# Attention in a convolution block: the last row-sum addition of a group behind the group's eviction, group-norm steps and position sums at other places

## The chip, the core and the metric

The kernel runs on one core of one Trainium2 chip. Its time is the device time of one execution in microseconds (us), the median of three runs; lower is better. The core has a matrix engine (TensorE, PE in the profile, with its weight loads as PEld), a vector engine (VectorE, DVE), a scalar engine (ScalarE, ACT), a general engine (GpSimd, POOL) and a queue engine (SyncE, SP). Each engine works through its own instructions in the order in which they were built, and waits on semaphores for the others.

## The reference

The input is 8 images of 512 channels, 32 x 32 positions, float32. The layer is a group norm, a block of convolutions with two attentions in it, and a residual:

```python
t = cbs(x, cv1_w, cv1_bn, 0)                 # 1x1 convolution, batch norm, silu
ys = [t[:, :C], t[:, C:]]                    # C = 256
for i in range(N):                           # N = 2 blocks
    yi = ys[-1]
    z = cbs(yi, m_cv1_w[i], m_cv1_bn[i], 1)  # 3x3 convolution
    z = bot_attention(z, m_qkv_w[i], m_rw[i], m_rh[i])
    z = silu(bn_eval(conv2d(z, m_cv2_w[i], 0), m_cv2_bn[i]))
    ys.append(yi + z)
return cbs(concatenate(ys, axis=1), cv2_w, cv2_bn, 0)
# bot_attention: 4 heads of 64 channels over 1024 positions
q, k, v = conv2d(x, qkv_w, 0)
r = rw + rh                                  # position sums, one 1024-vector per channel
a = softmax(einsum('bhdi,bhdj->bhij', q, k + r) * HD ** (-0.5))
out = einsum('bhij,bhdj->bhdi', a, v)
# whole layer: x + block(group_norm(x))
```

## The kernel before

The 8 images are worked on in four **rounds** (`p` = 0 to 3) of two images, a **first** and a **second** one. A round runs the 3x3 convolution of block 0 for both images, then project and attention of the first image, then of the second, and the same for block 1, and then the last 1x1 convolution. That makes 16 attentions, each by `attention_fast`. While they run, the other engines prepare what comes next: the group norm of the next round's images, tiles of the next convolution, weights for later rounds.

**One attention** has 4 groups (two heads by one half of the query positions); a group has 8 tiles of 128 keys, taken two at a time, so 4 steps. In a step PE makes the logits of two key tiles (L1037, `l_ps`), ACT the exponentials (L1041, `pt`), DVE adds them up over the keys into `acc` (L1055 for the first two tiles of a group, L1057 after that), and PE multiplies the step before by v into `av_ps` (L1071). At the end of a group ACT copies one half of `av_ps` into `z` (L1078) and DVE adds the other half to it (L1079): this is the **eviction**. There is one buffer for `av_ps`, so the next group's first product with v waits for it.

A **border** is the place between two groups, border 1 to 3 in each attention. There the engines' orders are: PE makes the logits of the new group's first step, the products with v of the old group's last step, the logits of the new group's second step, and then the products with v of the new group's first step. DVE does the old group's last additions, the eviction, and the new group's first addition L1055.

**Sums.** The softmax's denominators are the sums of `acc` over the partitions, made by PE with a matrix of ones (L1089, `s_ps`). In most attentions groups 0 and 1 are summed together at border 2, ahead of the products with v of group 2's first step, and groups 2 and 3 after the attention. Five attentions (both of round 0's block 0, and the second image's of block 0 in rounds 1 to 3) sum group 2 alone at border 3 as well. `acc` has two buffers.

**Hooks.** `behind` maps a place in the attention, group or (group, step), to a function that issues some instruction of other work behind that step's addition. `NORM_A` is the list of places at which the next round's first image goes through a step of its group norm (`group_norm`) during the first image's block 0 attention of rounds 1 and 2: four steps of statistics (DVE, L718 and L719), one for the mean over a group of channels (two small matmuls on PE, L725 `gm_ps`, then DVE L734 to L737), one for the deviation (`gv_ps`), and four that scale a tile of x (ACT, L809).

**Position sums.** `make_r(0)` adds `rw` and `rh` into four tiles (DVE, L217) and stores them to HBM from the POOL queue (L221). They are read by the projections of block 0 from round 1 on. Round 0 issues them in `middle()`, between the two images' attentions of block 1, with DVE's work of the second image's projection (L989 to L1006).

`tc.issue_after(ins)` makes what is issued inside it stand behind `ins`; a scheduler sets the rest of each engine's order when the program is built.

Of the kernel before, what the change touches and what calls it, by code (L numbers as in the profile page):

```python
# [47 lines left out]
ALU = mybir.AluOpType  # L48
# [13 lines left out]
def kernel(  # L62
# [16 lines left out]
    nc = tc.nc  # L79
# [7 lines left out]
    NJ = HW // P  # L87
# [121 lines left out]
    def make_r(n, raw=None):  # L209
        if raw is not None:  # L210
            with tc.issue_after(s.last_exp[0].ins):
                turn_r(n, raw)
            yield
        for c in range(NM):
            for half in range(NH):
                r = act.tile([P, ROWS, F], F32, tag="t", name="r_new", bufs=4)
                tt(  # L217
                    r, rw_sb[:, n, c].unsqueeze(1).to_broadcast([P, ROWS, F]),
                    rh_sb[:, n, c, ts(half, ROWS)].unsqueeze(2).to_broadcast([P, ROWS, F]), ALU.add,
                )  # L220
                put_r[0] = nc.gpsimd.dma_start(r_dram[n][c][:, ts(half, HALF)], r.rearrange("p h w -> p (h w)"))  # L221
                yield
# [268 lines left out]
    def stages(act, small, ps_big, ps_av, n_pt):  # L491
# [522 lines left out]
        def attention_fast(qkv, ao, at, behind, at_once=False, apart=False):  # L1014
# [4 lines left out]
            groups = [(c, half) for c in range(NM) for half in range(NH)]  # L1019
            steps = [(g, j) for g in range(len(groups)) for j in range(NJ)]  # L1020
            PAIR = 2
            pairs = [steps[i : i + PAIR] for i in range(0, len(steps), PAIR)]
            pts, accs, avs = {}, {}, {}

            def logits(pair):
                g, j0 = pair[0]
# [23 lines left out]
            def add_up(pair):  # L1050
                g, j0 = pair[0]
                pt = pts[pair[0]]
                if j0 == 0:
                    accs[g] = act.tile([P, 2, HALF], F32, tag="acc", name="acc", bufs=2)
                    return nc.vector.tensor_tensor(accs[g], pt[0], pt[1], ALU.add)  # L1055
                for i in range(PAIR):
                    ins = nc.vector.tensor_tensor(accs[g], accs[g], pt[i], ALU.add)  # L1057
                return ins

            def times_v(pair):  # L1060
# [95 lines left out]
            s_drams, rss, evicted = {}, {}, [None]  # L1156
            for i in range(len(pairs) + 1):
                if i < len(pairs):
                    added = logits(pairs[i])
                    g, at_q = divmod(i, NQ)  # L1160
                    with tc.issue_after(added.ins):
                        if at_q == NQ - 2 and g - 1 in batch:
                            gs = batch[g - 1]
                            rss[gs] = spread(gs, s_drams[gs])
                        if i == 1:
                            later()
                        if at_q == 1 and g - 2 in batch:
                            scale_all(batch[g - 2])
                if i > 0:
                    g, j0 = pairs[i - 1][0]  # L1170
                    if j0 == 0 and g - 1 in batch:
                        s_drams[batch[g - 1]] = sums(batch[g - 1])
                    times_v(pairs[i - 1])
                    if i < len(pairs) and accs.get(pairs[i][0][0], 0) is None:
                        with tc.issue_after(evicted[0].ins):
                            before = behind.get(("border", pairs[i][0][0]), lambda: None)() or evicted[0]
                        with tc.issue_after(before.ins):
                            added = add_up(pairs[i])
                    with tc.issue_after(added.ins):
                        behind.get(g if j0 == 0 else (g, j0 // PAIR), lambda: None)()  # L1180
# [3 lines left out]
            g = len(groups) - 1  # L1184
            if not at_once:
                gs = batch[g]
                if apart:
# [3 lines left out]
                    evicted=evicted[0], added=added,  # L1191
# [492 lines left out]
    with tc.issue_after(first.ins), tc.issue_after(made.ins):  # L1684
        multiplied, _, applied, powered = next(norm)
# [149 lines left out]
    for p in range(NP):  # L1835
# [125 lines left out]
                        calls[key].append(extra[key])  # L1961
            return {key: (lambda fs: lambda: [f() for f in fs])(fs) for key, fs in calls.items()}

        NORM_A = ((0, 1), (0, 3), (1, 1), (1, 2), 2, (2, 1), (2, 2), (2, 3), 3, (3, 1))
        NORM_B = ((0, 1), (0, 3), (1, 1), (1, 2), 2, (2, 1), (2, 2), (2, 3), 3, (3, 1), (3, 2), (3, 3))
        extra = {}
        if p == 0:
# [4 lines left out]
            r_steps = make_r(1, load_r(1))  # L1972
# [3 lines left out]
        behind = hooks(() if p == 0 else NORM_A, {0: 2} | {i: 1 for i in range(1, 9)}, extra) | {NG: begin_cv1(0, Y1[0], ia + 2)}  # L1976
        if p == 0:
            behind[NG + 1] = lambda: nxt.go_on()
        end = s.attention_fast(qkv, z[:, :, 0], at_of(ia, 0), behind, at_once=p == 0)
# [115 lines left out]
        behind = hooks(NORM_B, {0: 1, 1: 1, 4: 1}, {key: step_part for key in at_keys})  # L2095
# [81 lines left out]
        behind = {NG: start_b}  # L2177
# [15 lines left out]
        def middle():  # L2193
            end.spread()
            end.scale()
            s.m2(1, z[:, :, 0], Y2[0], lambda oc, half: img(y3a[half][:, oc, :]))
            if p == 0:
                with tc.issue_after(end.evicted.ins):
                    for _ in make_r(0):
                        pass  # L2200
            if more:
                nxt.finish()
                nxt.keep()
            s.exp_table()
# [6 lines left out]
        if p == 0:  # L2211
            ws = {name: load_ws(name) for name in ("21", "22", "11", "12")}
            new, sums1, sums2 = make_ws(ws)
# [27 lines left out]
        a1, a1_more, a2, a3 = s.strassen(ia, w_of, top, tags_a, tile_of)  # L2241
        behind = {NG: a1}
        if p == 0:
            behind |= {0: sums1, 1: sums2}
        end = s.attention_fast(qkv, z[:, :, 1], at_of(ib, 1), behind)
        y3b = act.tile([P, NH, NM, HALF], F32, tag="v", name="y3b")
        end.sums()
# [134 lines left out]
```

## Time and profile before

| | |
|---|---|
| time, median of 3 runs | 2251.07 us (2250.76 to 2251.08) |
| profiled execution, from the first to the last instruction (span) | 2246.8 us |
| PE busy | 2200.9 us (98%) |
| DVE busy | 1728.7 us (77%) |
| ACT busy | 1099.6 us (49%) |
| POOL busy | 224.4 us (10%) |
| granted TensorE clock, mean | 0.999 |
| chain that ended last | PE 85%, DVE 11%, ACT 1%, issue 1%, DMA 1% |

The profile is of one execution. Its span is 4.3 us under the median of the timed runs, which also hold what lies before the first and behind the last instruction. A row of the timeline gives the start in us from the span's start, the duration in us (of all instructions merged into the row), engine, line, operation, output<-inputs, shapes and count, and in brackets how long the engine stood idle before it and what ended that. A row of the waits gives who waited for what, us in total, times, and the longest in us. Matmul rows overlap: a float32 matmul shows as two records, and the ends are modelled, so the time that PE needs is read from start to start.

### The profile page before, as it was taken

How to read it: one execution, taken by the hardware profiler on the slowest of the kernel's cores; microseconds unless marked ns; L12 is line 12 of the kernel's file. 1: busy time of each engine (PE TensorE's matmuls, PEld its weight loads, DVE VectorE, ACT ScalarE, POOL GpSimd, SP SyncE). 2: the span in 40 equal slices, each digit the busy share in tenths (PEclk: the TensorE clock that was granted, in tenths of full speed). 3: DMA queues.
4: the chain of work that ended last, by engine and by line, in shares of the span. 5: the costliest groups of instructions: out<-in, count | busy, mean ns of one | idle time of the engine just before them, and what ended most of it. 6: DMA issues, size and time to landing. Idle time of an engine off the chain costs nothing.

```text
span 2246.8 us, 40264 instructions
## 1 busy us (share of the span) xinstructions
PE 2200.9 (98%) x16346; PEld 1080.6 (48%) x16346; DVE 1728.7 (77%) x2648; ACT 1099.6 (49%) x1332; POOL 224.4 (10%) x417
## 2 busy tenths in 40 slices
PE   7999999999999999999999999999999999999998
PEld 3653437343474444634447343654344734473443
DVE  7988879878678688877857868986794868797652
ACT  7554653644225665456324666455622455335533
POOL 4322210000220000000021000000012000000001
PEclk9999999999999999999999999999999999999999
DMA  9854447321581324511257141532136611350214
GB/s 273 308 163 150 150 151 261 109 78 45 140 275 49 118 81 145 183 58 67 67 159 261 30 169 35 197 116 77 58 76 173 233 39 34 102 198 30 67 50 112
DMA packets 134309, 285.60 MB, mean 127 GB/s; under 512 B 33540, under 2 KB 61184, under 8 KB 133092
## 3 DMA queue, kind: packets, MB, share of 16 engines
q1 hardware_dynamic: 102212, 197.34, 26.7%
q0 software_dynamic: 31904, 85.61, 13.3%
q8 instruction: 131, 2.15, 0.4%
q14 instruction: 62, 0.51, 0.1%
HBM read 214.86 MB, written 68.03 MB: 126 GB/s over the span
## 4 chain that ended last, share of the span: by engine, by line
PE 85%; DVE 11%; issue 1%; ACT 1%; DMA 1%; SPq 0%; POOL 0%; DVEq 0%; ACTq 0%; POOLq 0%
PE av_ps L1071 18%; PE l_ps L1037 18%; PE c L1305 9%; PE c_ps L653 7%; PE c_new L1305 6%; PE p_ps L916 6%; PE ps L523 5%; PE m_ps L1285 5%; PE x_ps L1405 4%; PE p_ps L922 3%; PE s_ps L1089 1%; DVE acc L1057 1%; DVE c_e L680 1%; PE p_ps L886 1%; DVE c_t L673 1%
## 5 line engine op out<-in xcount | busy, mean ns | idle before, releaser
L1041 ACT ACTIVATE pt<-l_ps 128x1024 f32<-128x1024 f32 x512 | 495.5, 1023 | 332.1 <-PE l_ps L1037 218.8
L1057 DVE TENSOR_TENSOR acc<-acc,pt 128x1024 f32<-128x1024 f32 x384 | 469.6, 1223 | 44.6 <-ACT pt L1041 16.2
L1071 PE MATMUL av_ps<-pt,vT 64*64 64x512 f32 x4096 | 484.8, 590 | 5.2 <-DVE z L1079 4.9
L1037 PE MATMUL l_ps<-q,kr 64*64 64x512 f32 x4096 | 486.3, 590 | 3.0 <-ACT pt L1041 1.9
L1071 PEld LDWEIGHTS av_ps<-pt,vT 64*64 64x64 f32 x4096 | 156.3, 133 | 284.8 <-issue 233.5
L1037 PEld LDWEIGHTS l_ps<-q,kr 64*64 64x64 f32 x4096 | 157.5, 133 | 273.2 <-issue 247.0
L653 PE MATMUL c_ps<-v_in,u 128*64 128x128 f32 x4320 | 239.1, 273 | 2.5 <-issue 2.5
L653 PEld LDWEIGHTS c_ps<-v_in,u 128*64 128x64 f32 x4320 | 235.8, 137 | 9.4 <-issue 9.4
L1285 PE MATMUL m_ps<-z,m_sb 128*128 128x512 f32 x256 | 114.1, 593 | 0.0
L658 ACT COPY c_m<-c_ps 128x512 f32<-128x512 f32 x48 | 28.0, 584 | 170.1 <-PE c_ps L653 140.8
L916 PE MATMUL p_ps<-t_z,sq 128*128 128x512 f32 x224 | 107.0, 595 | 0.0
L1079 DVE TENSOR_TENSOR z<-av_ps,z 128x512 f32<-128x512 f32 x64 | 44.1, 689 | 79.1 <-ACT z L1078 79.1
L1055 DVE TENSOR_TENSOR acc<-pt 128x1024 f32<-128x1024 f32 x64 | 78.0, 1219 | 18.0 <-PE s_ps L1089 11.2
L495 ACT ACTIVATE t<-m_ps,bh,sh 128x512 f32<-128x512 f32 x64 | 46.3, 773 | 91.2 <-PE m_ps L1285 91.2
L916 PE MATMUL p_ps<-z,sq 128*128 128x512 f32 x168 | 80.1, 604 | 5.3 <-ACT z L495 5.2
L1355 POOL DMA_DIRECT2D c_out<-in_x_dram x56 | 50.2, 954 | 293.2 <-ACT c_out L495 288.5
L1285 PEld LDWEIGHTS m_ps<-z,m_sb 128*128 128x128 f32 x256 | 47.8, 190 | 56.8 <-issue 52.5
L1147 DVE TENSOR_TENSOR z<-z,rs 128x512 f32<-128x512 f32 x64 | 42.3, 686 | 27.4 <-DMA rs<-r_dram 27.2
L495 ACT ACTIVATE c_out<-cz,bh,sh 128x512 f32<-128x512 f32 x14 | 16.8, 1301 | 89.1 <-DVE cz L1382 89.1
L495 ACT ACTIVATE z<-z,bh,sh 128x512 f32<-128x512 f32 x64 | 47.6, 804 | 25.8 <-DVE z L704 25.2
L1405 PE MATMUL x_ps<-t_x,sw 128*128 128x512 f32 x128 | 55.9, 592 | 0.0
L922 PEld LDWEIGHTS p_ps<-sq,z 128*128 128x128 f32 x336 | 42.7, 191 | 26.6 <-issue 12.7
(313 smaller groups left out, 3143.4 us busy)
## 6 DMA issues: line engine op xcount, KB each, us to landing
u<-u SPq DMA_DIRECT2D x135, 512.0 KB, 4.8
rs<-r_dram SPq DMA_DIRECT2D x126, 128.0 KB, 3.1
sq<-sq SPq DMA_DIRECT2D x42, 384.0 KB, 5.9
x<-in_x_dram SPq DMA_DIRECT2D x28, 512.0 KB, 7.0
r_in<-r SPq DMA_DIRECT2D x28, 512.0 KB, 4.9
y_in<-y SPq DMA_DIRECT2D x28, 512.0 KB, 4.4
c_out<-in_x_dram POOLq DMA_DIRECT2D x56, 256.0 KB, 5.1
out_dram<-c_out POOLq DMA_DIRECT2D x56, 256.0 KB, 3.3
```

Of the source, the lines that this page charges most:

```text
L495: silued[0] = nc.scalar.activation(dst, src, AF.Silu, scale=sh[:, k : k + 1], bias=bh[:, k : k + 1])
L523: last_product[0] = nc.tensor.matmul(ps[:, half, :], w_of(k), rhs_of(k, half), start=(k == begin), stop=(k == end))
L653: conv_product[0] = nc.tensor.matmul(to[o], us[cp][:, k, row, c, o], rhs, start=(k == 0), stop=(k == NM - 1),)
L916: nc.tensor.matmul(ps[:, o, :], w[:, o, :], rhs, start=not onto, stop=True, skip_group_check=onto)
L922: nc.tensor.matmul(v[:, ts(j, P)], rhs[:, ts(j, P)], w[:, 2, :], start=j == 0 and not onto, stop=True, skip_group_check=True,)
L1037: nc.tensor.matmul(ps[kh * HD : (kh + 1) * HD, hd, :], kr[r, c, o : o + HD], q[r, c, ts(half, HALF)], start=True, stop=True,)
L1041: last_exp[0] = exp = nc.scalar.activation(pt, ps, AF.Exp, scale=SCALE)
L1057: ins = nc.vector.tensor_tensor(accs[g], accs[g], pt[i], ALU.add)
L1071: nc.tensor.matmul(avs[g][hd * HD : (hd + 1) * HD, kh, :], vT[r, j, o : o + HD], pt[i][r, hd, :], start=(j == 0), stop=(j == NJ - 1),)
L1285: nc.tensor.matmul(pss[half][:, oc, :], m2_sb[:, n, k, ts(oc, P)], ao[:, k, ts(half, HALF)], start=(k == 0), stop=(k == NM - 1),)
L1305: nc.tensor.matmul(ps[:, o, :], w[:, k, ts(o, P)], rhs[part][:, c], start=(k == 0 and not onto), stop=(k == KB - 1), skip_group_check=onto,)
L1405: nc.tensor.matmul(ps[:, o, :], w[:, c, ts(o, P)], rhs[c], start=(c == 0 and not onto), stop=(c == 1), skip_group_check=onto,)
```

## The change

Three edits:

1. In `add_up` and at the borders: the last of a group's additions (the second key tile of step 4) is no longer issued with the other one, ahead of the eviction, but behind the eviction and ahead of the new group's first addition. This holds for groups 0 to 2 of each attention, 48 places in all. The last group of an attention keeps the old order.
2. `NORM_A`: the fourth statistics step goes from step 2 to step 3 of group 1, which puts it behind border 2, and the four scaling steps go one place later each. Mean and deviation keep their places.
3. `make_r(0)` leaves `middle()`; its four steps are hooks in round 0's last attention (second image, block 1), at (1,2), 2, (2,2) and 3.

```diff
-            pts, accs, avs = {}, {}, {}
+            pts, accs, avs, last_pt = {}, {}, {}, {}
...
-                for i in range(PAIR):
+                held_back = j0 + PAIR == NJ and g + 1 < len(groups)
+                for i in range(PAIR - held_back):
                     ins = nc.vector.tensor_tensor(accs[g], accs[g], pt[i], ALU.add)
+                if held_back:
+                    last_pt[g] = pt[-1]
                 return ins
...
                         with tc.issue_after(evicted[0].ins):
-                            before = behind.get(("border", pairs[i][0][0]), lambda: None)() or evicted[0]
+                            before = nc.vector.tensor_tensor(accs[g], accs[g], last_pt.pop(g), ALU.add)
+                        with tc.issue_after(before.ins):
+                            before = behind.get(("border", pairs[i][0][0]), lambda: None)() or before
                         with tc.issue_after(before.ins):
                             added = add_up(pairs[i])
...
-        NORM_A = ((0, 1), (0, 3), (1, 1), (1, 2), 2, (2, 1), (2, 2), (2, 3), 3, (3, 1))
+        NORM_A = ((0, 1), (0, 3), (1, 1), (1, 3), 2, (2, 1), (2, 3), 3, (3, 1), (3, 2))
...
             s.m2(1, z[:, :, 0], Y2[0], lambda oc, half: img(y3a[half][:, oc, :]))
-            if p == 0:
-                with tc.issue_after(end.evicted.ins):
-                    for _ in make_r(0):
-                        pass
             if more:
...
         if p == 0:
-            behind |= {0: sums1, 1: sums2}
+            r_steps = make_r(0)
+            behind |= {0: sums1, 1: sums2} | {at: lambda: next(r_steps) for at in ((1, 2), 2, (2, 2), 3)}
```

What the built programs' orders show (line numbers shift: the held-back addition is L1179, L1057 becomes L1058, L1079 becomes L1082, L1089 becomes L1092):

PE's order and SP's are the same in both programs. Of DVE at border 2 of round 1's first image, block 1 (acc: row sums, pt: exponentials, z: attention output, rc: reciprocals of the sums), before:

```order
L1057 TENSOR_TENSOR acc<-acc,pt 128x1024 x2
L1079 TENSOR_TENSOR z<-av_ps,z 128x512
L1055 TENSOR_TENSOR acc<-pt 128x1024
L1057 TENSOR_TENSOR acc<-acc,pt 128x1024 x4
L1131 RECIPROCAL rc<-sums_all 128x16
```

and now:

```order
L1058 TENSOR_TENSOR acc<-acc,pt 128x1024
L1082 TENSOR_TENSOR z<-av_ps,z 128x512
L1179 TENSOR_TENSOR acc<-acc,pt 128x1024
L1055 TENSOR_TENSOR acc<-pt 128x1024
L1058 TENSOR_TENSOR acc<-acc,pt 128x1024 x4
L1134 RECIPROCAL rc<-sums_all 128x16
```

One of the two additions ahead of the eviction now stands behind it, as the last one that `s_ps` needs.

In the first image's block 0 attention of round 1 (st, mv: statistics of x; gm: mean over a channel group), DVE from border 2 on is now as follows; before, the two BN_STATS and the BN_AGGR stood ahead of the eviction:

```order
L1058 TENSOR_TENSOR acc<-acc,pt 128x1024
L1082 TENSOR_TENSOR z<-av_ps,z 128x512
L1179 TENSOR_TENSOR acc<-acc,pt 128x1024
L1055 TENSOR_TENSOR acc<-pt 128x1024
L718 BN_STATS st<-x 128x6 x2
L1058 TENSOR_TENSOR acc<-acc,pt 128x1024
L719 BN_AGGR mv<-st 128x2
L1058 TENSOR_TENSOR acc<-acc,pt 128x1024
L734 COPY gm<-gm_ps 128x4
```

The last statistics, which `gm_ps` on PE reads, now come behind two more additions. ACT in the same attention from the end of group 2 on (L1041: exponentials, L809: scaling of x, COPY z: the eviction's first half), before:

```order
L1041 ACTIVATE pt<-l_ps 128x1024 x4
L809 ACTIVATE x<-x,shift,gr 128x1024
L1041 ACTIVATE pt<-l_ps 128x1024 x2
L809 ACTIVATE x<-x,shift,gr 128x1024
L1078 COPY z<-av_ps 128x512
L1041 ACTIVATE pt<-l_ps 128x1024 x2
```

and now:

```order
L1041 ACTIVATE pt<-l_ps 128x1024 x6
L809 ACTIVATE x<-x,shift,gr 128x1024
L1081 COPY z<-av_ps 128x512
L1041 ACTIVATE pt<-l_ps 128x1024 x2
L809 ACTIVATE x<-x,shift,gr 128x1024
L1041 ACTIVATE pt<-l_ps 128x1024 x2
```

Between the exponentials of group 2's last step and the copy of border 3 there is one scaling instead of two; the fourth scaling now stands behind the last exponentials and the load of the next function table.

DVE in the second image's projection of round 0, block 1 (r_new: position sums; kr, q, vT: operands of the coming attention), before; now the two L217 rows are gone from here, and the four additions stand one by one inside the attention that follows:

```order
L1293 TENSOR_TENSOR y_half<-t,ypad_67 128x512 x4
L217 TENSOR_TENSOR r_new<-rw_sb,rh_sb 128x512 x2
L989 TENSOR_TENSOR kr<-p_ps,u_z 128x512
L990 TENSOR_TENSOR q<-p_ps,u_z 128x512
L991 TENSOR_TENSOR vT<-p_ps,u_zv 128x4x128
L994 TENSOR_TENSOR kr<-kr,m_z 128x512
L217 TENSOR_TENSOR r_new<-rw_sb,rh_sb 128x512 x2
L995 TENSOR_TENSOR q<-q,m_z 128x512
```

## The prediction, made before the changed kernel was run

> **What bounds the kernel now.** I read the page first (busy times, clock, costliest groups), then PE's waits, then the timeline of PE, ACT and DVE around the borders and the moved work.
>
> ```profile
> span 2246.8 us, 40264 instructions
> PE 2200.9 (98%) x16346; PEld 1080.6 (48%) x16346; DVE 1728.7 (77%) x2648; ACT 1099.6 (49%) x1332; POOL 224.4 (10%) x417
> PEclk9999999999999999999999999999999999999999
> L1071 PE MATMUL av_ps<-pt,vT 64*64 64x512 f32 x4096 | 484.8, 590 | 5.2 <-DVE z L1079 4.9
> PE av_ps L1071 <- DVE z L1079: 4.9, 5, 1.6
> ```
>
> PE is busy 98% of the span at full clock, and its order is the same in both programs. So the time changes by PE's waits alone: those that go and those that come. The eviction (DVE z L1079), which the first edit brings forward, makes PE wait 5 times of 48 borders, 4.9 us in all. That is the most that edit can win, whatever the other 43 borders do.
>
> **Edit 1, what it wins.** Why only 5 times? At a usual border (here border 2 of round 1's first image, block 1) the eviction is held by ACT, not by the addition:
>
> ```profile
> 973.14 0.58 ACT L1078 COPY z<-av_ps 128x512 f32<-128x512 f32 x1 [0.63 <-PE av_ps L1071]
> 973.76 0.69 DVE L1079 TENSOR_TENSOR z<-av_ps,z 128x512 f32<-128x512 f32 x1 [0.33 <-ACT z L1078]
> 975.43 1.23 DVE L1055 TENSOR_TENSOR acc<-pt 128x1024 f32<-128x1024 f32 x1 [0.98 <-PE s_ps L1089]
> 974.72 1.07 PE L1089 MATMUL s_ps<-acc,ones 128*32 128x256 f32 x16
> 975.18 0.61 PE L1089 MATMUL s_ps<-acc,ones 128*32 128x256 f32 x8
> 975.72 1.52 PE L1071 MATMUL av_ps<-pt,vT 64*64 64x512 f32 x12
> ```
>
> The copy ends at 973.72 and the eviction starts 0.04 later, after DVE has idled 0.33. Taking an addition from ahead of it does not move it. It does move at border 1 of the second image's block 0 attention, where DVE is behind:
>
> ```profile
> 815.94 0.58 ACT L1078 COPY z<-av_ps 128x512 f32<-128x512 f32 x1 [0.57 <-PE av_ps L1071]
> 817.75 0.68 DVE L1079 TENSOR_TENSOR z<-av_ps,z 128x512 f32<-128x512 f32 x1
> 818.35 1.22 DVE L1055 TENSOR_TENSOR acc<-pt 128x1024 f32<-128x1024 f32 x1
> 819.48 1.28 DVE L718 BATCH_NORM_STATS2 st<-x 128x6 f32<-128x512 f32 x2
> 821.80 0.20 DVE L719 BATCH_NORM_AGGREGATE mv<-st 128x2 f32<-128x12 f32 x1
> 826.38 0.16 DVE L737 TENSOR_TENSOR dev<-dev,mv 128x4 f32<-128x4 f32 x1
> 818.49 1.95 PE L1071 MATMUL av_ps<-pt,vT 64*64 64x512 f32 x16 [0.90 <-DVE z L1079]
> 827.24 0.17 PE L725 MATMUL gv_ps<-dev,gmat 64*64 64x4 f32 x1
> ```
>
> The eviction could start at 816.55 instead of 817.75, and PE would not wait: 0.90 of idle, about 1.1 from start to start, since busy ends overlap the next start by some 0.2. The same border of round 2 idles about 0.5 (the 4.9 less twice 1.57, this 0.90 and a 0.34, which stand under edits 2 and 3), 0.7 start to start. Together 1.8. But the held-back addition is put in front of the norm's DVE work. Up to L737 DVE has no idle time: 1.20 earlier, 1.13 of addition more (818.35 to 819.48 is what one takes), so L737 still ends near 826.5, while PE wants `gv_ps` 1.1 earlier, at 826.1. It waits about 0.4 there, in both rounds: 0.8 goes back. In round 0's second image the same matmul is already the one that waits:
>
> ```profile
> 272.90 0.16 DVE L737 TENSOR_TENSOR dev<-dev,mv 128x4 f32<-128x4 f32 x1
> 273.20 0.23 PE L725 MATMUL gv_ps<-dev,gmat 64*64 64x4 f32 x2 [0.27 <-DVE dev L737]
> ```
>
> There the eviction is ACT's as usual, so DVE comes later by the whole 1.13, and PE with it. Term A: -1.8 + 0.8 + 1.1 = **+0.1**. Bounds: -1.8 if no `gv_ps` waits, +0.6 if these three waits are half a microsecond longer together.
>
> **Edit 1, what it costs.** The wait changes its place. The sums L1089 stand in PE's order ahead of the products with v of the new group, and they read `acc`, which is now complete only after the eviction. In the rows above the eviction starts at 973.76; the next DVE instruction follows 0.60 later (817.75 to 818.35) and an addition takes 1.22: it ends 1.83 after the eviction's start, and PE starts 0.06 after a DVE result (817.75 + 0.68, then 818.49). So `acc` is there at 973.76 + 1.89 = 975.65. Of the 16 records the first 8 belong to the older group, whose sum is long done; the other 8 start at 975.18. PE stands 0.47, and behind it everything. This is at border 2 of all 16 attentions: 16 x 0.47 = 7.5. In round 3's second image, block 0, DVE is late as well:
>
> ```profile
> 1899.95 0.68 DVE L1079 TENSOR_TENSOR z<-av_ps,z 128x512 f32<-128x512 f32 x1
> 1900.12 1.07 PE L1089 MATMUL s_ps<-acc,ones 128*32 128x256 f32 x16
> ```
>
> One addition less ahead, one more at the border before: I leave the eviction where it is, and `acc` comes at 1901.84 for a start at 1900.58; that is 1.26, 0.8 above the usual, and I take 0.7. Where group 2 is summed alone, all 8 records need the held-back addition:
>
> ```profile
> 846.55 0.69 DVE L1079 TENSOR_TENSOR z<-av_ps,z 128x512 f32<-128x512 f32 x1 [2.68 <-ACT z L1078]
> 847.51 0.64 PE L1089 MATMUL s_ps<-acc,ones 128*32 128x256 f32 x8
> 848.08 1.50 PE L1071 MATMUL av_ps<-pt,vT 64*64 64x512 f32 x10
> ```
>
> 846.55 + 1.89 = 848.44 against 847.51: 0.93, five times, 4.7. Term B: 7.5 + 0.7 + 4.7 = **+12.9**. Bounds from the 0.06 and 0.60 being 0.1 off either way at 21 places: 10.8 to 15.0. At the other 27 borders the addition fills DVE time that no PE instruction waits for, apart from the norm work of term A. What is later there by 1.1 is the new group's own additions; the exponentials get their buffers back a step or more before they need them.
>
> **Edit 2.** In the first image's block 0 attention of rounds 1 and 2, the two scalings (1.24 each) stand ahead of border 3's copy:
>
> ```profile
> 733.64 1.24 ACT L809 ACTIVATE x<-x,shift,gr 128x1024 f32<-128x1024 f32 x1 [1.80 <-POOL shift L803]
> 736.60 1.23 ACT L809 ACTIVATE x<-x,shift,gr 128x1024 f32<-128x1024 f32 x1
> 737.73 0.58 ACT L1078 COPY z<-av_ps 128x512 f32<-128x512 f32 x1
> 739.08 1.95 PE L1071 MATMUL av_ps<-pt,vT 64*64 64x512 f32 x16 [1.57 <-DVE z L1079]
> ```
>
> Here PE idles 1.57, 1.7 start to start. Now one scaling stands there, behind exponentials that come first: I expect the copy about 1.3 earlier against PE, and 0.4 of the wait left (bounds 0 and 1.7). Won: 1.3. But the mean's matmul keeps its place, and the statistics that it reads have moved behind the border:
>
> ```profile
> 723.02 1.23 DVE L1055 TENSOR_TENSOR acc<-pt 128x1024 f32<-128x1024 f32 x1 [0.98 <-PE s_ps L1089]
> 725.09 0.17 PE L725 MATMUL gm_ps<-mv,gmat 64*64 64x4 f32 x1
> ```
>
> DVE gets to L1055 at about 723.1 as before, since the held-back addition fills the 0.98. Behind it stand two BN_STATS, an addition and BN_AGGR, which elsewhere took 818.35 to 822.00, 3.65. So the statistics are there at 726.8, and PE, later by 0.47 itself, wants them at 725.56: it waits 1.25 (bounds 0 and 1.7). Term C: 2 x (-1.3 + 1.25) = **-0.1**, bounds -3.4 to +3.4.
>
> **Edit 3.** Round 0's second projection of block 1 has four more DVE instructions than round 3's, and the attention behind it is longer:
>
> ```profile
> 473.09 1.28 DVE L217 TENSOR_TENSOR r_new<-rw_sb,rh_sb 128x512 f32<-128x512 f32 x2
> 475.89 1.95 PE L1037 MATMUL l_ps<-q,kr 64*64 64x512 f32 x16
> 479.83 1.09 PE L1037 MATMUL l_ps<-q,kr 64*64 64x512 f32 x8 [0.62 <-DVE q L997]
> 496.24 1.95 PE L1071 MATMUL av_ps<-pt,vT 64*64 64x512 f32 x16 [0.34 <-DVE z L1079]
> 535.40 3.63 PE c L1305 x8
> 2097.38 3.66 PE L1037 MATMUL l_ps<-q,kr 64*64 64x512 f32 x32
> 2153.70 3.63 PE c L1305 x8
> ```
>
> From the first logits to the next stage 535.40 - 475.89 = 59.51, in round 3 2153.70 - 2097.38 = 56.32. I take the whole difference, **-3.2** (term D; the 0.34 at border 1 is in it), since in the new places DVE idles ahead of the eviction (0.33 in the usual border), takes over one addition's time there, and the last of the four follows border 3. Their stores go behind the stores of the weight sums in POOL's queue, and are read only in round 1. If that cover is gone, each of the four (0.64) can hold PE: bounds -3.2 and -0.6.
>
> **Sum:** 0.1 + 12.9 - 0.1 - 3.2 = +9.7; a PE that stood still restarts some hundredths late at two dozen places, so I write +10. The profiled span would go from 2246.8 to 2256.8, and the median, which was 4.3 above it, from 2251.1 to **2261**.
>
> **The rivals.** (1) *The sums do not wait, and it is faster.* The 0.98 that DVE idles ahead of L1055 at border 2 is nearly the size of the addition: it looks like free room. It decides at one point, whether `acc` is complete before the second half of the sums, 0.47 earlier than I count. Then B is gone and with it C's shift: 0.1 - 0.1 - 3.2, about -3.2 for 2247.9, and with no waits for `gm_ps` and `gv_ps` 2243. Against it: the eviction starts with the copy's end, and nothing in the change moves that. 4%.
> (2) *Gain and loss cancel.* If the waits at the sums are 0.2 and 0.5 instead of 0.47 and 0.93, B is 5.7 to 6.4 and the sum +3: 2254, within what can be told. 8%.
> (3) *The norm steps win as meant:* if `gm_ps` does not wait, C is -2.6: 2258.6. 12%.
> (4) *The position sums hold PE in their new place:* D is -0.6 or less: 2263.7. 9%.
> (5) *The clock.* If the new short stops let the granted clock halve for a step each, some 25 steps of 3.5 (56.32 / 16) would take twice as long: +88, 2339. The clock row shows no slice below 9 with stops up to 1.57 in it. 1%.
> The Trainium skill (TensorE: Matmul & The Clock Gate, Part 1, "A second HAM failure mode: psum-queue depth-cycling") speaks for rival 5: micro-idles between groups of matmuls made one kernel's clock swing. The same page ("Why this matters for your kernels") names idle gaps above about 3 us as what re-throttles; by that rule these stops, at most 1.3 each, cost no clock, and this trace agrees so far with a mean of 0.999.
>
> **How the numbers follow.** My forecast has 66%, the rivals 34%. The bounds give 2254 to 2270 if all fall on one side; adding half of them, and reaching to rivals 3 and 4, I say 2256.5 to 2266.5. What a measurement of this kernel can tell from no change is about 0.2%, 4.5 us. Slower than that (above 2255.6) are the forecast and rivals 3, 4 and 5: 88%. Same: rival 2, 8%. Faster: rival 1, 4%.
>
> **What would show it.** PE's waits should hold `s_ps` behind DVE `acc` 21 times, 0.4 to 1.3 each, some 12 us in all; today they hold none. `av_ps` behind DVE z should fall from 4.9 to about 1, `gm_ps` behind DVE mv should be new with some 1.2 twice, `gv_ps` behind DVE dev should grow. Round 0's last attention should lose its waits at the start. I am wrong if the sums start as early as before, or if the eviction starts before the copy lets it.

## The result and the profile after

The changed kernel takes 2264.59 us (median of 5 runs, 2263.16 to 2265.19) against 2251.07 (2250.76 to 2251.56, 5 runs): a ratio of 1.0059, 95% interval 1.0048 to 1.0070, or 13.5 us slower. Forecast were 2261 and a range of 2256.5 to 2266.5. The profiled execution has a span of 2263.3 us, 16.5 above that of before.

The page of the changed kernel: span, engines, granted clock, chain, and the group of the products with v.

```profile
span 2263.3 us, 40235 instructions
PE 2204.7 (97%) x16346; PEld 1079.7 (48%) x16346; DVE 1723.6 (76%) x2648; ACT 1101.7 (49%) x1332; POOL 222.6 (10%) x417
PEclk9999999999999999999999999999999999999999
PE 79%; DVE 15%; ACT 2%; issue 2%; DMA 1%; POOL 0%; SPq 0%; DVEq 0%; ACTq 0%; POOLq 0%
L1074 PE MATMUL av_ps<-pt,vT 64*64 64x512 f32 x4096 | 484.7, 590 | 0.2
```

PE, DVE, ACT and POOL have as many instructions as before, and the granted clock is nearly the same (0.998, before 0.999). In the chain that ended last DVE's share is now 15%, where it was 11%. The products with v hardly stand idle any more (5.2 us before, 4.9 of it for the eviction; 0.2 now). The waits of PE in the changed kernel (in all, times, longest) show what came for it:

```profile
PE gm_ps L725 <- DVE mv L719: 10.5, 3, 8.2
PE s_ps L1092 <- DVE acc L1179: 9.9, 21, 0.9
PE gv_ps L725 <- DVE dev L737: 3.4, 4, 1.4
PE m_ps L1290 <- DVE z L1150: 2.8, 3, 1.2
```

The second row is term B of the prediction: 21 waits of the sums for the held-back addition, the number forecast (9.9 us of idle time, where some 12 were forecast). The third and first are the norm's: `gv_ps` had 1.2 in 2 waits, and `gm_ps` one wait of 8.0 at the program's start, to which two of 1.15 have come. The fourth row the prediction does not have.

A usual border 2 now (round 1's first image, block 1, the one that the prediction showed):

```profile
979.58 0.59 ACT L1081 COPY z<-av_ps 128x512 f32<-128x512 f32 x1 [0.63 <-PE av_ps L1074]
980.20 0.69 DVE L1082 TENSOR_TENSOR z<-av_ps,z 128x512 f32<-128x512 f32 x1 [0.67 <-ACT z L1081]
980.81 1.22 DVE L1179 TENSOR_TENSOR acc<-acc,pt 128x1024 f32<-128x1024 f32 x1
981.16 0.64 PE L1092 MATMUL s_ps<-acc,ones 128*32 128x256 f32 x8
982.08 0.64 PE L1092 MATMUL s_ps<-acc,ones 128*32 128x256 f32 x8 [0.28 <-DVE acc L1179]
981.94 1.22 DVE L1055 TENSOR_TENSOR acc<-pt 128x1024 f32<-128x1024 f32 x1
982.65 1.09 PE L1074 MATMUL av_ps<-pt,vT 64*64 64x512 f32 x8
```

The copy ends at 980.17 and the eviction starts 0.03 later: it does not start earlier against the copy. DVE idles 0.67 ahead of it instead of 0.33, and has lost the 0.98 that it idled ahead of L1055. PE gets the complete `acc` 1.88 after the eviction's start (counted: 1.89), and the second half of the sums follows the first by 0.92, where it followed by 0.46 before. The row shows only 0.28 of this as idle, because the first half's shown end (981.80) lies 0.18 beyond the point at which the next one could have started. Attentions in which nothing else changed take 56.81 us instead of 56.33, which is 0.48. With group 2's sums alone (round 1's second image, block 0):

```profile
851.98 0.69 DVE L1082 TENSOR_TENSOR z<-av_ps,z 128x512 f32<-128x512 f32 x1 [3.53 <-ACT z L1081]
852.59 1.22 DVE L1179 TENSOR_TENSOR acc<-acc,pt 128x1024 f32<-128x1024 f32 x1
853.95 0.64 PE L1092 MATMUL s_ps<-acc,ones 128*32 128x256 f32 x8 [0.94 <-DVE acc L1179]
```

Here PE starts 1.97 after the eviction's start. Since PE's order is the same in both programs, its records can be matched one to one, and the distance between the two traces grows by 1.01 at this row: the stop costs 1.01, of which 0.94 shows as idle. Matched in the same way, border 2 costs about 0.46 in 14 attentions, and 1.01 at the late one of round 3. In round 0's first image, block 0, it costs 0.75; there, too, other DVE work stands ahead of the eviction.

**The row that was not forecast.** Behind the second image's block 1 attention in rounds 0, 1 and 2 the convolution goes on, and the scaled heads are multiplied with the output weights (`m_ps`). Round 1, before, on DVE and PE:

```profile
1083.39 3.70 PE L1305 MATMUL c<-y_in,ws 128*128 128x512 f32 x8
1087.40 0.68 DVE L1079 TENSOR_TENSOR z<-av_ps,z 128x512 f32<-128x512 f32 x1
1094.34 0.24 DVE L1131 RECIPROCAL rc<-sums_all 128x16 f32<-128x16 f32 x1
1100.37 0.69 DVE L1147 TENSOR_TENSOR z<-z,rs 128x512 f32<-128x512 f32 x1 [0.51 <-DMA rs<-r_dram]
1101.12 2.41 PE L1285 MATMUL m_ps<-z,m_sb 128*128 128x512 f32 x5
```

And after:

```profile
1080.15 1.22 DVE L1179 TENSOR_TENSOR acc<-acc,pt 128x1024 f32<-128x1024 f32 x1
1086.28 5.21 DVE L1058 TENSOR_TENSOR acc<-acc,pt 128x1024 f32<-128x1024 f32 x4
1091.41 2.35 DVE L1334 TENSOR_TENSOR t_in<-y_in 128x1024 f32<-128x1024 f32 x2
1090.80 3.70 PE L1310 MATMUL c<-y_in,ws 128*128 128x512 f32 x8
1095.95 0.69 DVE L1082 TENSOR_TENSOR z<-av_ps,z 128x512 f32<-128x512 f32 x1
1102.89 0.24 DVE L1134 RECIPROCAL rc<-sums_all 128x16 f32<-128x16 f32 x1
1109.00 0.69 DVE L1150 TENSOR_TENSOR z<-z,rs 128x512 f32<-128x512 f32 x1 [1.74 <-DMA rs<-r_dram]
1109.75 1.55 PE L1290 MATMUL m_ps<-z,m_sb 128*128 128x512 f32 x3 [1.17 <-DVE z L1150]
```

Counted from the stage's first matmul, the last eviction comes 5.15 us later instead of 4.01, the reciprocal 12.09 instead of 10.95: both are late by 1.14, one addition. Behind the addition held back at border 3 DVE has no gap above 0.11 us up to the reciprocal, so the addition's time is carried along. The reciprocal starts a chain through HBM (`r_dram`, `rs`) to the scaling and to `m_ps`, which had no slack before: the scaling ended at 1101.06, `m_ps` started at 1101.12. Round 0 waits the same 1.16 there, round 2 0.45. Matched with the trace before, the three stages lose 1.43, 1.22 and 0.72, together 3.4.

### The profile page after: what moved, and what is told of

It reads as the page before. It is cut to its first block, busy times and chain, and to the rows that moved or that the text cites. A ratio compares the mean times of both kernels' runs of the same rounds, so it can differ in the third digit from the quotient of the medians.

```text
span 2263.3 us, 40235 instructions
## 1 busy us (share of the span) xinstructions
PE 2204.7 (97%) x16346; PEld 1079.7 (48%) x16346; DVE 1723.6 (76%) x2648; ACT 1101.7 (49%) x1332; POOL 222.6 (10%) x417
## 4 chain that ended last, share of the span: by engine, by line
PE 79%; DVE 15%; ACT 2%; issue 2%; DMA 1%; POOL 0%; SPq 0%; DVEq 0%; ACTq 0%; POOLq 0%
PE av_ps L1074 17%; PE l_ps L1037 16%; PE c_ps L653 7%; PE c L1310 7%; PE p_ps L916 6%; PE c_new L1310 6%; PE ps L523 5%; PE m_ps L1290 5%; PE x_ps L1410 4%; PE p_ps L922 3%; DVE acc L1058 2%; DVE acc L1179 1%; PE s_ps L1092 1%; DVE z L1082 1%; ACT z L1081 1%
## 5 line engine op out<-in xcount | busy, mean ns | idle before, releaser
L1041 ACT ACTIVATE pt<-l_ps 128x1024 f32<-128x1024 f32 x512 | 495.9, 1023 | 337.0 <-PE l_ps L1037 283.0
L1058 DVE TENSOR_TENSOR acc<-acc,pt 128x1024 f32<-128x1024 f32 x336 | 410.9, 1223 | 37.7 <-ACT pt L1041 13.9
L1082 DVE TENSOR_TENSOR z<-av_ps,z 128x512 f32<-128x512 f32 x64 | 44.2, 690 | 126.9 <-ACT z L1081 126.9
L1055 DVE TENSOR_TENSOR acc<-pt 128x1024 f32<-128x1024 f32 x64 | 78.0, 1220 | 6.7 <-ACT pt L1041 6.7
L1179 DVE TENSOR_TENSOR acc<-acc,pt 128x1024 f32<-128x1024 f32 x48 | 58.4, 1216 | 0.0
```

Of the source, the lines that this page charges most:

```text
L1041: last_exp[0] = exp = nc.scalar.activation(pt, ps, AF.Exp, scale=SCALE)
L1179: before = nc.vector.tensor_tensor(accs[g], accs[g], last_pt.pop(g), ALU.add)
```

## The experiments

Times are compared with the kernel before on the same chip: 2251.44 us for the first four kernels, 2250.78 for the next four, 2250.52 for the last two. "The attentions" are the sum of the 16 stretches from an attention's first logits to the first matmul behind it: 917.54 us in the profile before, 928.47 in the changed kernel's.

### Each edit alone, and the last border

**The addition alone** (the second and third edit undone):

```diff
-        NORM_A = ((0, 1), (0, 3), (1, 1), (1, 3), 2, (2, 1), (2, 3), 3, (3, 1), (3, 2))
+        NORM_A = ((0, 1), (0, 3), (1, 1), (1, 2), 2, (2, 1), (2, 2), (2, 3), 3, (3, 1))
+            if p == 0:
+                with tc.issue_after(end.evicted.ins):
+                    for _ in make_r(0):
+                        pass
-            behind |= {0: sums1, 1: sums2} | {at: lambda: next(r_steps) for at in ((1, 2), 2, (2, 2), 3)}
+            behind |= {0: sums1, 1: sums2}
```

> Edit 1 alone (the held-back addition), the norm steps and the position sums as in the kernel before. If edits 1 and 3 act apart from each other, this is the changed kernel's 2264.6 plus the 3.1 that round 0's last attention won (59.51 to 56.90 with 0.48 of new wait in it), plus some 0.4 for edit 2: about 2268. Rival, edit 1 costs only the idle time that the profile shows before the sums (9.9): 2261. In the profile: s_ps behind DVE acc 21 times, gv_ps waits as in the changed kernel, m_ps behind DVE z three times, av_ps behind DVE z left only at the two borders that ACT's scalings hold.

Measured: 2263.32 us, 1.0053 (1.0039 to 1.0067), 11.9 above before. The attentions are 928.79. So this edit makes nearly the whole loss. Round 0's last attention takes 59.42 us, as it does with the position sums in their old place, but the first images' block 0 attentions of rounds 1 and 2 take 57.8 us, 0.9 *less* than in the changed kernel. The time expected, 2268, was missed: with edit 1 in place edit 2 costs 0.9 in each of two attentions, where I had counted it as even, and that takes up most of the 2.5 us that round 0's last attention is longer. The rival's 2261 was missed too: a usual border costs 0.48, not the 0.28 of idle time. The attentions together are only 0.3 above the changed kernel's; that the time lies 1.6 nearer to its before is within the intervals.

Why does the first edit alone gain at border 3 of the first images, where the prediction has ACT's scalings hold the eviction? The wait of 1.57 is 0.54 here and 0.52 in round 2, and the products start 1.03 and 1.05 sooner against the matmuls around them. The scaling waits for a small step on POOL (`shift`), and in the kernel before this step stands beside the last addition of group 2. Here that addition is held back (rows of before, then of this kernel):

```profile
730.96 2.55 DVE L1057 TENSOR_TENSOR acc<-acc,pt 128x1024 f32<-128x1024 f32 x2 [0.74 <-ACT pt L1041]
732.34 1.27 POOL L803 TENSOR_SCALAR shift<-shift 128x4 f32<-128x4 f32 x1
```

```profile
738.99 1.22 DVE L1058 TENSOR_TENSOR acc<-acc,pt 128x1024 f32<-128x1024 f32 x1 [0.86 <-ACT pt L1041]
740.36 0.23 POOL L803 TENSOR_SCALAR shift<-shift 128x4 f32<-128x4 f32 x1
```

Beside the addition the step shows 1.27, behind it 0.23, and the first scaling starts 0.03 to 0.04 after its end in both (733.64 and 740.63). The first two edits thus win the same wait: once the first has taken 1.03 of it, the scalings' new place wins only 0.46 more, while the statistics' new place costs 1.33. That is the 0.9.

**The norm steps alone** (the kernel before with the new `NORM_A`):

> Edit 2 alone. My theory: the scaling that leaves border 3 wins 1.5 in each of two attentions (1.73 to 0.24), and the statistics behind border 2 make gm_ps wait: L1055 at 723.02 as before, 3.65 later the statistics at 726.67, PE wants them at 725.09, so 1.6 each. Sum +0.2 to +0.4: 2251.4. Rival, the steps win as meant and gm_ps waits only because of the held-back addition: -3.0, 2248.1.

Measured: 2251.64 us, 1.0002 (0.9993 to 1.0011). The two attentions take 58.66 us instead of 58.36. PE does not wait for the eviction at border 3 there any more, but for the mean, in the timeline of this kernel:

```profile
727.61 0.22 PE L725 MATMUL gm_ps<-mv,gmat 64*64 64x4 f32 x2 [1.57 <-DVE mv L719]
```

The wait needs no held-back addition. It comes from the statistics' new place, and eats what the scalings' new place wins.

**The position sums alone** (the kernel before with the third edit):

> Edit 3 alone. Round 0's last attention should take 56.3 to 56.5 instead of 59.5, and nothing else change: 2251.1 - 3.1 = 2248.0. Rival, the moved additions are late next at the attention's end, where DVE works ahead of the reciprocals: 0.6 of it comes back at m_ps, 2248.6; or the whole gain does, 2251.

Measured: 2249.31 us, 0.9992 (0.9983 to 1.0001). The attention takes 57.74 us: 1.77 of the 3.2 are won. The waits ahead of it are gone, but not the one at border 1, which was 0.34 before. DVE and PE in this kernel:

```profile
489.76 5.21 DVE L1057 TENSOR_TENSOR acc<-acc,pt 128x1024 f32<-128x1024 f32 x4
494.89 0.68 DVE L1079 TENSOR_TENSOR z<-av_ps,z 128x512 f32<-128x512 f32 x1
495.63 1.95 PE L1071 MATMUL av_ps<-pt,vT 64*64 64x512 f32 x16 [1.19 <-DVE z L1079]
```

PE now comes earlier to a DVE that is still behind, and stands 1.19 at the eviction. In the changed kernel the fourth addition of that row stands behind the eviction, and the wait is not there: its attention takes 56.90, of which 0.48 are the sums' wait. So -3.1 is what the two edits give together.

**No addition held back at border 3 of block 1's attentions** (otherwise the changed kernel):

```diff
-                held_back = j0 + PAIR == NJ and g + 1 < len(groups)
+                held_back = j0 + PAIR == NJ and g in hold
-        end = s.attention_fast(qkv, z[:, :, 1], at_of(ib, 1), behind)
+        end = s.attention_fast(qkv, z[:, :, 1], at_of(ib, 1), behind, hold=(0, 1))
```

(and the same for the first image; `hold` is (0, 1, 2) elsewhere)

> The changed kernel, but in the eight attentions of block 1 border 3 keeps its old order (both additions ahead of the eviction); no sums stand at that border there. The prediction had priced the addition at these borders at nothing. Theory now: it stays in DVE's queue until after the attention, in front of the reciprocals, and m_ps waits for it three times, 1.16, 1.17 and 0.45 (the stages behind these attentions are 3.3 longer once a 0.87 wait that comes and goes is left out): 2264.6 - 3.3 = 2261.3, m_ps behind DVE z gone. Rival, these waits are a matter of how fast the small DMAs landed in that execution: 2264.6, waits still there.

Measured: 2262.04 us, 1.0047 (1.0033 to 1.0060), 10.6 above its before where the changed kernel is 13.5 above its own. The attentions are the same (928.50), and the wait for the scaling is gone from the list of PE's waits. In round 1 of this kernel:

```profile
1087.84 3.70 PE L1312 MATMUL c<-y_in,ws 128*128 128x512 f32 x8
1098.78 0.25 DVE L1134 RECIPROCAL rc<-sums_all 128x16 f32<-128x16 f32 x1
1104.62 0.69 DVE L1150 TENSOR_TENSOR z<-z,rs 128x512 f32<-128x512 f32 x1 [0.31 <-DMA rs<-r_dram]
1105.45 5.33 PE L1292 MATMUL m_ps<-z,m_sb 128*128 128x512 f32 x12
```

The reciprocal is back at 10.94 after the stage's first matmul. That the carried addition makes the `m_ps` waits is shown. How long they are still differs from execution to execution: the kernels that hold the addition there show 2.1 to 3.0 us in three waits, and some that do not show one short wait, of 0.4 at most.

### The place of the sums, and of the statistics

**The sums behind the new group's first products with v** (otherwise the changed kernel):

```diff
+                    times_v(pairs[i - 1])
                     if j0 == 0 and g - 1 in batch:
                         s_drams[batch[g - 1]] = sums(batch[g - 1])
-                    times_v(pairs[i - 1])
```

> The changed kernel, but at the borders the sums are issued behind the new group's first products with v instead of ahead of them. Theory (it is the place of the sums in PE's order that makes the change slow: they want acc while the held-back addition still runs): the products give DVE 1 us or more, the 21 waits of s_ps for DVE acc (9.9 us shown, some 13 from start to start) are gone or below 0.1 each, most attentions are back at 56.3 to 56.4, the time falls by about 12 to 2252 or 2253. What stays: m_ps for DVE z 2.8, gm_ps for DVE mv two of about 1.1, gv_ps for DVE dev 3.4. Rival (the addition in the eviction's neighbourhood is slow wherever the sums stand: the products then reach their bank before the eviction, or L1055 waits for the later sums and DVE stays late): av_ps waits for DVE z 0.3 to 0.5 at 16 or more borders, attentions at 56.7 or more, time at 2260 or above.

Measured: 2254.79 us, 1.0018 (1.0009 to 1.0027): 4.0 above before. The 21 waits are gone, the usual attentions are at 56.33 again, and the attentions together at 917.79, 10.7 less than in the changed kernel. So the sums' place in PE's order carries term B. But the time stayed 2 to 3 us above what I expected. This kernel shows where, at border 2 of round 1's first image in block 0:

```profile
726.20 1.07 PE L1092 MATMUL s_ps<-acc,ones 128*32 128x256 f32 x16
726.91 1.23 DVE L1055 TENSOR_TENSOR acc<-pt 128x1024 f32<-128x1024 f32 x1 [1.56 <-PE s_ps L1092]
730.72 0.22 PE L725 MATMUL gm_ps<-mv,gmat 64*64 64x4 f32 x2 [1.58 <-DVE mv L719]
```

The sums no longer wait, but the new group's first addition waits 1.56 for the sums' read of an older `acc` (there are two buffers), and everything on DVE behind it is later: `gm_ps` waits 1.58 instead of 1.15, and the last sums behind three second images' block 0 attentions wait 0.95, 0.40 and 0.4 for additions, which they did not before.

**The statistics back in their old place** (otherwise the changed kernel):

```diff
-        NORM_A = ((0, 1), (0, 3), (1, 1), (1, 3), 2, (2, 1), (2, 3), 3, (3, 1), (3, 2))
+        NORM_A = ((0, 1), (0, 3), (1, 1), (1, 2), 2, (2, 1), (2, 3), 3, (3, 1), (3, 2))
```

> The changed kernel with the norm's statistics step of the first images put back to its old place, so that only the two scalings stand one step later. Theory (gm_ps waits because the statistics went behind the border, and the scalings need not take them along): the two new waits of gm_ps for DVE mv (1.15 each, 1.3 from start to start) are gone, the row falls from 10.5 to 8.2 or 8.3, the two attentions fall from 58.72 to 57.4, the time by 2.6 to 2262.0. Rival (the statistics ahead of the border make DVE late for the eviction there): gm_ps does not wait but av_ps does for DVE z by about 1 at those two borders, attentions at 58.4 to 58.7, time unchanged at 2264.6.

Measured: 2262.19 us, 1.0048 (1.0034 to 1.0062). `gm_ps` has its one wait of 8.0 again, the two attentions take 57.37 us instead of 58.72, 2.7 us in both. In the time against its own before it is 2.1 less than the changed kernel. Confirmed: only the scalings needed to move.

**The scalings and the position sums, no addition held back.** The same `NORM_A`, the third edit, and `hold=()`.

> The kernel before with no addition held back, the position sums in the attention, and only the two scalings one step later, the statistics in their old place. Theory (the second and third edits carry a gain of their own once the statistics stay): the two attentions of the first images fall from 58.36 by 1.3 to 57.1, round 0's last attention from 59.51 to 57.74 as with the position sums alone, no s_ps and no m_ps wait; 2251.4 - 2.6 - 1.8 = 2247.0. Rival (the eviction at border 3 waits for something other than the scalings): attentions stay at 58.3, time 2249.3 as with the position sums alone.

Measured: 2246.49 us, 0.9982 (0.9973 to 0.9991): faster than before by 4.3. The two attentions take 56.88 us, a gain of 1.48 each.

**The sums behind, the statistics back, border 3 of block 1 free**: all three losses found so far taken out of the changed kernel.

> The changed kernel with all three losses that the runs have shown taken away together: the sums behind the first products, the statistics in their old place, no addition held back at the last border of block 1's attentions. Theory (these three are the whole of it): s_ps waits at no border, gm_ps only 8.0 as before, m_ps not at all; attentions 912.6 in all against 917.5 before, gv_ps 3.0 and the late last sums of three second images in block 0 (1.0, 0.5, 0.5) stay; time 2248.5, below before by 2. Rival (a fourth loss that the single runs hide, from DVE's additions being later everywhere): time 2252 or above, with waits of PE for DVE that none of these has.

Measured: 2258.07 us, 1.0033 (1.0020 to 1.0045). The rival holds, and I had worked out 2248.5. The attentions are 922.44, and the loss is in four of them: the first images' block 0 in rounds 1 and 2 take 61.55 and 59.85 us, those of block 1 57.45 and 57.44. Round 1's first one, on DVE and PE:

```profile
724.67 1.23 DVE L1055 TENSOR_TENSOR acc<-pt 128x1024 f32<-128x1024 f32 x1 [1.56 <-PE s_ps L1092]
728.47 0.15 DVE L734 COPY gm<-gm_ps 128x4 f32<-128x4 f32 x1
728.66 1.23 DVE L1058 TENSOR_TENSOR acc<-acc,pt 128x1024 f32<-128x1024 f32 x1
730.07 1.22 DVE L1058 TENSOR_TENSOR acc<-acc,pt 128x1024 f32<-128x1024 f32 x1
731.21 0.16 DVE L737 TENSOR_TENSOR dev<-dev,mv 128x4 f32<-128x4 f32 x1
731.51 0.22 PE L725 MATMUL gv_ps<-dev,gmat 64*64 64x4 f32 x2 [2.78 <-DVE dev L737]
```

L1055 waits 1.56 for the sums, and two more additions have come to stand between the norm's short steps L734 and L737, so PE waits 2.78 for `gv_ps`. In block 1 the lateness meets the eviction at border 3: `av_ps` waits 0.9. The sums behind the products are thus no free repair in these kernels: they take the wait from PE and give it to DVE. Which of the other two changes lets this lateness through to PE was not tried one by one.

### Where the held-back addition wins

**Held at border 1 of round 1's and 2's second image, block 0, alone** (added to the faster kernel above):

```diff
-        end = s.attention_fast(qkv, z[:, :, 1], at_of(ib, 0), behind, apart=True)
+        end = s.attention_fast(qkv, z[:, :, 1], at_of(ib, 0), behind, apart=True, hold=(0,) if more and not direct else ())
```

> As the run with the scalings and the position sums and no addition held back, but the last addition is held behind the eviction at one border only: border 1 of the second image's block 0 attention in rounds 1 and 2, where the eviction was 1.2 late and no sums stand behind it. Theory (the first edit wins only where DVE itself keeps the eviction waiting): av_ps does not wait there (0.90 and 0.5 shown, 1.1 and 0.7 from start to start), gv_ps for DVE dev takes 0.4 of it back in each; the two attentions fall from 58.42 and 58.07 by 0.6 and 0.3 or more, 1.0 together; no s_ps wait for acc; time 1.0 below the run without any hold, 2246.0. Rival (the addition put in front of the norm's work costs as much as the eviction wins): gv_ps waits 0.9 or more at each, the two attentions stay within 0.2 of before, time 2247.

Measured: 2246.09 us, 0.9980 (0.9971 to 0.9989). The two attentions take 57.85 us each, 0.2 less than without, and the time is 0.4 less where I expected 1.0. In round 1 one wait replaces the other, first the row without the held-back addition, then, of this kernel, the row with it:

```profile
815.54 1.95 PE L1074 MATMUL av_ps<-pt,vT 64*64 64x512 f32 x16 [0.55 <-DVE z L1082]
```

```profile
824.65 0.23 PE L725 MATMUL gv_ps<-dev,gmat 64*64 64x4 f32 x2 [0.34 <-DVE dev L737]
```

The eviction's wait had already fallen from 0.90 to 0.55 there without any addition held back. In the kernel before and in the one with the norm steps alone, DVE's last addition ahead of this eviction starts only behind ACT's copy, after 0.46 of idle time; in the two kernels with the position sums moved and no addition held back here it does not wait for the copy. Why it does in the first two, these runs do not tell. A gain of 0.4 is within what a measurement can tell from none.

**Held at border 1 of round 0's last attention as well:**

```diff
-        end = s.attention_fast(qkv, z[:, :, 1], at_of(ib, 1), behind)
+        end = s.attention_fast(qkv, z[:, :, 1], at_of(ib, 1), behind, hold=(0,) if p == 0 else ())
```

> As the run with the addition held at border 1 of two attentions, and held besides at border 1 of round 0's last attention, where the position sums now stand and av_ps waits 1.18 for DVE z. Theory (a held-back addition wins where DVE is late for the eviction and no sums follow): that wait goes, the attention falls from 57.74 to 56.4, the row av_ps for DVE z is gone, time 1.3 lower, 2244.8. Rival (DVE stays late, and the wait goes on to the next border or to the sums at border 2): s_ps waits for DVE acc there, or av_ps at border 2, attention at 57.3 or more, time 2246.

Measured: 2244.62 us, 0.9972 (0.9960 to 0.9983), 5.9 below before and the fastest of all these kernels. The attention takes 56.41 us instead of 57.74. In this kernel three additions stand ahead of the eviction and one behind it, and PE's list has no wait of `av_ps` left:

```profile
489.81 3.88 DVE L1058 TENSOR_TENSOR acc<-acc,pt 128x1024 f32<-128x1024 f32 x3
493.60 0.69 DVE L1082 TENSOR_TENSOR z<-av_ps,z 128x512 f32<-128x512 f32 x1
494.20 1.22 DVE L1181 TENSOR_TENSOR acc<-acc,pt 128x1024 f32<-128x1024 f32 x1
```

## Why the prediction was right, and where it was not

By the prediction's terms, from the attentions' lengths in the two profiles:

| term | forecast | measured |
|---|---|---|
| A, evictions won against `gv_ps` | +0.1 | +0.7 |
| B, sums behind the held-back addition | +12.9 | +13.5 |
| C, norm steps | -0.1 | -0.2 |
| D, position sums | -3.2 | -3.1 |
| sum in the attentions | +9.7 | +10.9 |
| `m_ps` behind three attentions | not counted | +3.4 |

10.9 is 928.47 - 917.54. B is 14 usual borders of 0.48 (0.46 at the sums and 0.02 just behind them), 0.8 in round 0's first attention, 1.0 at the late border, and five single sums of 1.0. C is twice 58.72 - 58.36 - 0.48. D is 56.90 - 0.48 - 59.51. A is what then remains: +1.1 in round 0's second image and -0.2 in each of rounds 1 and 2. 3.4 is from the matched traces; the row of waits shows 2.8 of it as idle. Together 14.3, against 13.5 between the medians and 14.4 between the two profiles from the first logits to the end.

- **What bounds the kernel** held: PE's order did not change, and the difference is PE's waits.
- **Term B** held in its mechanism and its count, and the runs show it: with the sums behind the products the 21 waits are gone. The size was 0.6 short: a single sum cost 1.0 and not 0.93, since PE started 1.97 after the eviction's start and not 1.89; round 0's first border cost 0.3 more than a usual one, and the late one 0.2 less than I took.
- **Term A** held for round 0's second image to the hundredth: `gv_ps` waits 1.40, the 0.27 of before and 1.13. In rounds 1 and 2 I counted 0.4 each; it is 0.70 and 0.35 of idle time, 0.88 and 0.53 from start to start, 1.4 instead of 0.8. That is the 0.6 that A is off.
- **Term C** came out, with its two halves as said: `gm_ps` waits 1.15 and costs 1.3 (1.25 forecast), and the scalings alone win 1.48 (1.3 forecast, with 0.4 of the eviction's wait left; hardly any was). That the held-back addition by itself takes 1.03 of the same wait, through POOL, the prediction did not see; it does not show in C, because the scalings' new place leaves nothing of the wait.
- **Term D** came out, but its reason was incomplete. I had put the 0.34 at border 1 into the gain because DVE idles at a usual border. Round 0's last attention is not a usual one: alone, the third edit leaves a wait of 1.19 at its border 1 and wins 1.8. The first edit takes that wait away, which I had not said.
- **The step that failed** is "At the other 27 borders the addition fills DVE time that no PE instruction waits for". At border 3 of block 1's second images in rounds 0, 1 and 2 it fills no idle time: it is carried through 23 us of DVE work with hardly a gap to the reciprocal that `m_ps` depends on. I followed the addition to the attention's end and not to the next place where PE waits for DVE. From start to start it makes 3.4 of the 4.6 us by which the terms come out above the forecast 9.7, and the run that takes it out is 2.9 us nearer to its before. The result lies in the range all the same: the range was made wide for other terms, which came out near their forecast. For this term that is luck.
- **The step from the span to the median** used the 4.3 by which the median lay above the profiled span. In the changed kernel it is 1.3. The execution profiled before had a short start: PE gets one of the first matmuls of block 0 after a wait of 1.76, and of 3.48 in the changed kernel's profile, before anything that the change touches (rows of before, then of after). The spans differ by 16.5 and the medians by 13.5: the later start is 2.0 of the 3.0 between these two, and the other 1.0 is not traced.

```profile
75.05 3.71 PE L653 MATMUL c_ps<-v_in,u_new 128*64 128x128 f32 x64 [1.76 <-DVE v_in L607]
```

```profile
77.08 3.71 PE L653 MATMUL c_ps<-v_in,u_new 128*64 128x128 f32 x64 [3.48 <-DVE v_in L607]
```

Of the rivals, (1), (2) and (4) are refuted by the waits and by round 0's last attention, (3) by `gm_ps`; that (3) would have held with the statistics left where they were is shown by the run that puts them back. (5), the clock, did not happen: 28 new stops on PE of up to 1.17 us, and one that grew from 0.27 to 1.40, leave a mean granted clock of 0.998. The Trainium skill (TensorE: Matmul & The Clock Gate, "Why this matters for your kernels") says that it is longer gaps, above about 3 us, that re-throttle. The trace agrees with it without testing it, since these stops are all shorter; the one longer stop between matmuls, the 3.48 us of `c_ps` above, left the granted clock at 1.00 in the 8 us behind it. The trace before, too, had longer stops between matmuls (2.2 us) than the 1.57 that the prediction names. The warning of micro-idles on the same page of the Trainium skill did not come true for stops this short and far apart.

## What to carry to other kernels

Moving work behind an instruction that sets a buffer free helps where the engine itself keeps that instruction waiting: here at three of 48 borders. Holding the addition at these three, with the norm's scalings and the position sums moved, gives 2244.6 us against 2250.5; without any addition held the same moves give 4.3 us, so the three borders are worth some 1.6. Holding it at all 48 borders costs 12. At two more borders it helps by a detour, through a step on POOL that ran beside the addition, and the moved scalings win that wait without it. Before moving it, look for the next reader of the result that is now late, on every engine, and follow a late engine through its queue to the first place where another one waits for it, even if that is 20 us and a stage away. Where several steps are moved together, ask of each one whether it has to go along: the statistics did not, and took back what the scalings won.

## What the runs showed of the hardware

A stop of PE costs more than the idle time shown before the row: 0.28 shown was 0.46 to 0.48 from start to start, since a sums' matmul's shown end lies 0.18 beyond the point at which the next one can start; 0.94 ahead of a single sum was 1.01. The start of the program is not the same in every execution: the first logits come between 145.98 and 148.28 us in the profiles of these kernels, which do not differ up to that point, and the wait of `c_ps` shown above is the largest part of it. Differences of 2 us between two profiled spans therefore mean nothing here until that start is taken off.

A small POOL step (`shift`, 128x4) shows 1.27 or 1.28 us wherever a DVE addition stands beside it, and 0.23 us where none does: six of these kernels each way, at two places in each. POOL's spans are rough, but where ACT's scaling waits for the step (the kernel before, the first edit alone, the third edit alone) it starts 0.04 us behind the step's shown end. What the two engines share there, the runs do not show.
